# Cross-attention in layer 1 of a decoder: order of two score passes, and the places of the work around them

## The chip, the cores and the metric

The kernel is one program on one core of a Trainium2 chip. It is timed in microseconds (us) on the device, as the median of several executions; lower is better. A core has TensorE (matmuls, profile name PE, its weight loads PEld), VectorE (DVE), ScalarE (ACT), GpSimd (POOL) and SyncE (SP), each with a queue that it works through in order, and DMA engines that move data between the memories. Matmul results land in PSUM, which has banks of 512 float32 per partition; VectorE and ScalarE read them from there.

## The reference

The kernel computes a decoder of two layers on x of shape 4 x 512 x 512, each layer being self-attention, cross-attention and a feed-forward part with a layer norm after each. The change is in layer 1's cross-attention and in the preparation of the weights of the feed-forward part behind it. Cut to what is computed there:

```python
q = (x @ Wq).reshape(b, n, 32, 16)
k, v = jnp.split(ctx @ Wkv, 2, axis=-1)          # each reshaped to (b, ctx_n, 32, 16)
q = apply_axial_rope(q, pos_map)
k = apply_axial_rope(k, ctx_pos_map)
logits = jnp.einsum('bqhd,bkhd->bhqk', q, k) * scale
w = jax.nn.softmax(logits, axis=-1)
attn = jnp.einsum('bhqk,bkhd->bqhd', w, v)
x = layernorm(x + attn.reshape(b, n, 512) @ Wout + bout)

def quant_weight(w):                              # w_gate, w_up, w_down of the feed-forward part
    scale = jnp.mean(jnp.abs(w)) + EPS
    return jnp.clip(jnp.round(w / scale), -1.0, 1.0), scale
```

## The kernel before, in words

`l1_xattn` works on 4 batches (b) of 512 queries and 512 keys. The 32 heads of 16 channels are taken four at a time: a group `g` (32 in all) holds four heads, each in a strip of 32 partitions, of which 16 rows carry the head. Two groups make an `M` (16 in all, four to a batch), which share one projection of queries and keys. The scores are computed twice. `first_pass` (line 1178) makes scores with the queries along the partitions, and `row_maxes` (line 1182, VectorE) takes the negated maximum of each row. When the maxima of a group are there, `turn_maxes` transposes them (line 1187) and VectorE adds them to the queries as one more row (line 1188), so that `second_pass` (line 1194) makes scores with the keys along the partitions from which the maxima are already taken off. `exponentials` (line 1198, ScalarE) is then the plain exponential from PSUM to SBUF, and `values` (line 1205) multiplies it with the values and, by a column of ones, sums it.

The main loop in `run` has a step for each quarter (128 rows) of a group, 128 real steps in all, with a lead-in and an end. Each step has two halves. A half does the first pass for two of the four strips of the quarter five steps ahead, and the second pass for the other two strips of the present quarter. Each pass of a half takes one buffer of the pool `ps_b`, two banks wide; the pool has three buffers, handed out in turn, so a buffer is free for its third next user when VectorE's row maxes or ScalarE's exponential has read it. All other PSUM tiles of this stage come from the pool `ps_m`, two buffers of one bank, and one of them is held by the sum over four quarters that `values` builds up.

TensorE, VectorE and ScalarE keep the order in which the loop writes their instructions (`manual_schedule`); GpSimd and SyncE are put in order by the scheduler of the framework. The loop writes down, in each step, the two halves, and beside them what the dictionary `todo` holds for it. `plan(step, place, f, ...)` fills it: EARLY stands after the first half ahead of `values` of the step before, MIDDLE after those values, LATE after the second half. The entries that matter here:

- `project_queries`, `project_keys`: lines 1126 and 1140 on TensorE, copied out by ScalarE (1132, 1144), always LATE; `swap` and `rotate` then turn them by DMAs and GpSimd (1151 to 1161); `queries` (1166, ScalarE) and `keys` (1171, VectorE) mask them.
- `turn_residual`: transposes of the batch's x (1107), copied by ScalarE, and the bias added by GpSimd (1111).
- `prep_values`: the values' projection (line 160 is the helper `mm`), copied by ScalarE (1116).
- `gather` (ScalarE 1213 and 1214 for even groups, VectorE 1218 and 1219 for odd ones), `invert_sums` (transposes at 1225, reciprocals at 1229 on VectorE, a copy at 1231 on ScalarE) and `normalise` (transposes at 1238, product at 1243): the softmax's division.
- `out_projection`: one half of one tile of 128 rows in two parts of four matmul records each (1251), added to x by VectorE (1256), followed by the tile's statistics (219, 220); after a batch's last one GpSimd computes the inverse roots in a chain of small operations (227 to 234), and `normalise_tile` (239) uses them on VectorE.
- `quantized`: the three weights of the feed-forward part. In each of four chunks of 1 MB, loaded by SyncE (144), `add_up` sums the absolute values (1044); later `scale_of` adds the eight partial sums up on VectorE (1049) and over the partitions with a matmul (1051); then the chunks are loaded again and `round_off` scales half a chunk on VectorE (1062), clamps it on GpSimd (1063) and narrows it to bfloat16 on ScalarE (1064). Chunks take their buffers from the pool of ten weights, so a load waits until one is free.

Of the last real steps, those from 123 on have no first pass left. After the loop, the projections of batch 3 (entries of steps 130 to 137) and the feed-forward part follow.

Of the kernel before, what the change touches and what calls it, by code (L numbers as in the profile page):

```python
# [13 lines left out]
ALU = mybir.AluOpType  # L14
AX = mybir.AxisListType
# [71 lines left out]
def decoder_kernel(ctx: ExitStack, tc: tile.TileContext, a: dict, out: bass.AP):  # L87
# [21 lines left out]
    V, A, G, PE = nc.vector, nc.scalar, nc.gpsimd, nc.tensor  # L109
# [8 lines left out]
    def small(n, tag, bufs=2):  # L118
        return sp.tile([P, n], F32, tag=tag, name=tag, bufs=bufs)
# [15 lines left out]
    def psb():  # L135
        return pools["ps_b"].tile([P, 2, 512], F32, tag="b", name="ps_b")
# [33 lines left out]
    ones = cp.tile([P, P], F32, tag="ones", name="ones")  # L170
# [857 lines left out]
    def quantized(plan, name, n, sums_at, scale_at, rounds_at):  # L1028


        src = rows(a[name])
        per = 2048 // n
        got = {}

        def chunk(c):
            got["w"] = load(src[:, per * c:per * (c + 1), :], (per, n))

        def half(w, i):
            return w.rearrange("p k n -> p (k n)")[:, 1024 * i:1024 * i + 1024]

        def add_up(c, i):
            if c == 0 and i == 0:
                got["part"] = small(8, "part", 1)
            V.tensor_reduce(got["part"][:, 2 * c + i:2 * c + i + 1], half(got["w"], i), AX.X, ALU.add,
                            apply_absolute_value=True)

        def scale_of():
            row = small(1, "one", 8)
            V.tensor_reduce(row, got["part"], AX.X, ALU.add)
            ps = pst()  # L1050
            PE.matmul(ps[:, :1], lhsT=ones, rhs=row, start=True, stop=True)
            scale = cp.tile([P, 1], F32, tag=f"ws_{name}", name="ws")
            V.tensor_scalar(scale, ps[:, :1], 1.0 / (F * INNER), Q_EPS, ALU.mult, ALU.add)
            got["inv"] = cp.tile([P, 1], F32, tag=f"wi_{name}", name="wi")
            V.reciprocal(got["inv"], scale)
            wq = got["wq"] = [weight((2 * per, n), BF16) for _ in range(2)]
            quant[name] = chunks(wq[0]) + chunks(wq[1]), scale

        def round_off(c, i):
            w = half(got["w"], i)  # L1060
            dst = half(got["wq"][c // 2][:, per * (c % 2):per * (c % 2 + 1), :], i)
            V.tensor_scalar(w, w, got["inv"], ROUND, ALU.mult, ALU.add)
            G.tensor_scalar(w, w, ROUND + 1.0, ROUND - 1.0, ALU.min, ALU.max)
            A.activation(dst, w, AF.Copy, bias=-ROUND)

        for c in range(4):
            for at, f in ((sums_at, add_up), (rounds_at, round_off)):
                plan(at + 4 * c - 2 + (c == 0 and at == sums_at), LATE, chunk, c)
                for i in range(2):
                    plan(at + 4 * c + 2 * i, LATE, f, c, i)  # L1070
        plan(scale_at, EARLY, scale_of)


# [7 lines left out]
    def l1_xattn():  # L1081
# [92 lines left out]
        def first_pass(g, qi, half, s):  # L1174
            q, k = qk["q", g], qk["k", g]
            for j in range(2):
                i = 2 * half + j
                PE.matmul(s[:, j, :], lhsT=q[strip(i), tk(qi)], rhs=k[strip(i), :], start=True, stop=True)  # L1178

        def row_maxes(g, qi, half, s):  # L1180
            at = maxes[g % 2][:, qi, :].rearrange("p (i c) -> p i c", c=32)
            V.tensor_reduce(at[:, 2 * half:2 * half + 2, 16 * (1 - g % 2)], s, AX.X, ALU.max, negate=True)  # L1182
# [82 lines left out]
        def plan(step, place, f, *args):  # L1265
            todo.setdefault((step, place), []).append((f, args))
# [4 lines left out]
        for M in range(4 * B):  # L1271
            b, m, t0 = M // 4, M % 4, 8 * M
            if M:
                q, turn_q, turn_k = (-17, -13, -11) if M == 1 else (-21, -16, -13)
                for i in range(4):
                    plan(t0 + q + i, LATE, project_queries, M, i // 2, i % 2)
                plan(t0 + turn_q, EARLY, rotate, "q")
                for i in range(2):
                    plan(*(-5, EARLY) if M == 1 else (t0 - 17 + i, LATE), project_keys, M, i)
                plan(t0 + turn_k, EARLY, rotate, "k")  # L1280
            for par in range(2):
                plan(t0 - 10 + 2 * par if M else -9, EARLY, queries, M, par)
                plan(t0 - 7 + par if M else -9, EARLY, keys, M, par)
            for g in (2 * M, 2 * M + 1):
                plan(4 * g - 1, EARLY, turn_maxes, g)
                plan(4 * g + 4, MIDDLE, gather, g)
            if m == 0:
                if b:
                    plan(t0 - 23, EARLY, load_batch, b)
                    plan(t0 - 17, EARLY, angles)  # L1290
                    for k, x in enumerate(((-25, MIDDLE), (-23, EARLY), (-22, EARLY), (-21, MIDDLE))):
                        plan(t0 + x[0], x[1], turn_residual, b, k)
                for t, x in enumerate(((-3, MIDDLE), (-1, MIDDLE), (-1, MIDDLE), (1, EARLY))):
                    plan(t0 + x[0], x[1], prep_values, b, t)
            plan(t0 + 9 - (M == 4 * B - 1), LATE, invert_sums, M)
            plan(t0 + 10 - (M == 4 * B - 1), LATE, normalise, M)
            if m < 3:
                continue


            whole, pairs, norms = ((11, MIDDLE), (13, EARLY), (21, EARLY), (23, MIDDLE), (25, EARLY),
                                   (26, EARLY), (27, MIDDLE), (29, EARLY)), (), (33, 35, 37, 39)
            if b == B - 2:
                whole, pairs, norms = whole[:2], (19, 21, 23, 27, 29, 31), (34, 35, 36, 37)
            elif b == B - 1:
                whole, norms = [(10 + i, LATE) for i in range(8)], (18,) * 4
            for i, x in enumerate(whole):
                for part in range(2):
                    plan(t0 + x[0], x[1], out_projection, b, i // 2, i % 2, part)
            for i, x in enumerate(pairs, len(whole)):  # L1310
                for part in range(2):
                    plan(t0 + x + part, LATE, out_projection, b, i // 2, i % 2, part)
            for i in range(4):
                plan(t0 + norms[i], LATE, normalise_tile, b, i)
        for name, n, steps in (("L1_ffn_gateT", INNER, (2, 17, 19)), ("L1_ffn_upT", INNER, (35, 53, 54)),
# [22 lines left out]
        def run():  # L1338
            open_pools({"pp": (1, False), "ps_b": (3, True), "ps_m": (2, True)})
            st["wo"] = load(rows(a["L1_xattn_Wout"]), (4, F))  # L1340

            vv.extend(prob(f"vv{t}", [16, 48], 1) for t in range(4))
            for x in vv:
                G.memset(x[:, :, 16:32], 1.0)
            maxes.extend(prob(f"maxes{i}", [4, P], 1) for i in range(2))
            for x in maxes:
                G.memset(x, 0.0)

            N = 32 * B

            with tc.manual_schedule(engines={nc.tensor.engine, nc.vector.engine, nc.scalar.engine}):
                for step in range(min(x for x, _ in todo), max(x for x, _ in todo) + 1):
                    ahead, now, past = step + 5, step, step - 1
                    for half in range(2):
                        if 0 <= ahead < N:
                            s1 = psb()
                            first_pass(ahead // 4, ahead % 4, half, s1)
                        if 0 <= now < N:
                            s2 = psb()
                            second_pass(now // 4, now % 4, 1 - half, s2)  # L1360
                        if 0 <= ahead < N:
                            row_maxes(ahead // 4, ahead % 4, half, s1)
                        if 0 <= now < N:
                            exponentials(now // 4, now % 4, 1 - half, s2)
                        if half == 0:
                            for f, args in todo.get((step, EARLY), ()):
                                f(*args)
                            if 0 <= past < N:
                                values(past // 4, past % 4)
                            for f, args in todo.get((step, MIDDLE), ()):  # L1370
                                f(*args)
                    for f, args in todo.get((step, LATE), ()):
                        f(*args)
# [127 lines left out]
```

## Time and profile before

| what | value |
|---|---|
| median of 3 executions | 2916.74 us (2912.76 to 2916.99) |
| profiled execution, its own time | 2925.97 us |
| its span, first to last instruction | 2924.2 us |
| granted TensorE clock, mean | 0.983 |
| the stage of the edited loop | about 1970 to 2690 us of the span |
| busy in that stage (720 us) | TensorE 690.6, VectorE 458.5, ScalarE 366.2, GpSimd 198.5 |
| row maxes, line 1182 | 256 of 1.223 us |
| exponentials, line 1198 | 256 of 1.023 us |
| narrowing, line 1064 | 24 of 1.057 us |

A row of instructions names the line of the kernel, the engine, the operation, what it writes and reads with sizes, how often, the busy time in us and the mean in ns, and after a bar the idle time of the engine just before it with what ended that. A float32 matmul of the kernel appears as two records. A row of waits names who waited, for whom, and total us, times and longest. Records of TensorE that belong to different strips run at the same time and are counted once in busy time.

### The profile page before, as it was taken

The page shows a single profiled execution, that of the slowest core. Times are in us where ns is not written, and L with a number is a line of the kernel's source. Part 1 is how long each engine was busy: PE and PEld are TensorE (multiplying, and loading weights), DVE is VectorE, ACT ScalarE, POOL GpSimd, SP SyncE. Part 2 cuts the span into 40 slices and gives each one's busy share as a digit, 9 for nine tenths or more (in the row PEclk, how much of TensorE's full clock was granted, in tenths as well). Part 3 has the DMA queues.
Part 4 walks back from the last instruction along what each step waited for, and adds up shares of the span by engine and source line. Part 5 has one row for each costly group of instructions (what it writes and reads, how often), then busy time and mean ns, then how long its engine had stood idle before and what let it go on. Part 6 is the DMA issues. An engine that isn't in the chain of part 4 may idle for free. (4 is left out here: it accounts for less than half of the span.)

```text
span 2924.2 us, 30438 instructions
## 1 busy us (share of the span) xinstructions
PE 2763.2 (94%) x11434; PEld 1347.8 (46%) x11434; DVE 1757.1 (60%) x3551; ACT 1046.8 (36%) x1929; POOL 425.0 (15%) x436
## 2 busy tenths in 40 slices
PE   8999999998998889999999999999999999998987
PEld 3444444565665345555555555553334334334443
DVE  4565564553111476767667666756656666565998
ACT  2333342333221122232233223234555554554443
POOL 3000000042002100111101101123333232211000
PEclk9999999999999899999999999999999999999999
DMA  9700000004322120000000001111111020010000
GB/s 386 278 15 1 15 4 27 23 29 137 101 85 97 35 87 1 1 0 1 1 1 1 1 0 44 58 47 38 56 55 58 37 86 27 12 51 1 15 15 30
DMA packets 61128, 142.76 MB, mean 49 GB/s; under 512 B 6537, under 2 KB 26010, under 8 KB 54818
## 3 DMA queue, kind: packets, MB, share of 16 engines
q1 hardware_dynamic: 54818, 123.80, 11.8%
q0 software_dynamic: 6144, 16.79, 1.6%
q8 instruction: 99, 1.62, 0.2%
q14 instruction: 67, 0.55, 0.1%
HBM read 84.73 MB, written 47.45 MB: 45 GB/s over the span
## 5 line engine op out<-in xcount | busy, mean ns | idle before, releaser
L1182 DVE TENSOR_REDUCE maxes<-ps_b 128x2 f32<-128x1024 f32 x256 | 312.6, 1223 | 212.0 <-PE ps_b L1194 113.8
L160 PE MATMUL ps_m<-w,attnT 128*128 128x512 f32 (+1 forms) x992 | 391.8, 547 | 9.7 <-DVE x L313 9.7
L1198 ACT ACTIVATE PT<-ps_b 128x1024 f32<-128x1024 f32 x256 | 260.3, 1023 | 237.0 <-PE ps_b L1194 236.9
L1178 PE MATMUL ps_b<-k,q 32*128 32x512 f32 x1024 | 287.0, 642 | 6.8 <-ACT PT L1198 6.8
L1194 PE MATMUL ps_b<-q,k 32*128 32x512 f32 x1024 | 285.5, 642 | 1.4 <-DVE maxes L1182 1.4
L933 PE MATMUL ps_m<-xT,w 128*128 128x512 f32 x512 | 261.4, 594 | 0.0
L313 DVE TENSOR_TENSOR x<-x,ps_m 128x512 f32<-128x512 f32 x128 | 87.8, 687 | 284.5 <-PE ps_m L160 257.1
L160 PEld LDWEIGHTS ps_m<-w,attnT 128*128 128x128 f32 x736 | 141.2, 195 | 177.3 <-issue 162.8
L950 ACT ACTIVATE P<-ps_s,nmax 128x512 f32<-128x512 f32 (+3 forms) x256 | 135.4, 529 | 234.9 <-DVE nmax L948 233.8
L946 PE MATMUL ps_s<-k,q 128*128 128x512 f32 (+3 forms) x512 | 183.3, 441 | 19.1 <-POOL q L906 17.4
L906 POOL TENSOR_TENSOR q<-tmp 128x512 f32<-128x512 f32 x64 | 82.0, 1281 | 765.8 <-DVE tmp L905 731.2
L978 PE MATMUL ps_m<-PT,v 128*128 128x512 f32 (+3 forms) x512 | 162.8, 441 | 4.0 <-DVE PT L966 4.0
L370 ACT ACTIVATE P<-ps_s,nmax 128x512 f32<-128x512 f32 x128 | 88.5, 693 | 203.5 <-DVE nmax L368 203.5
L957 DVE TENSOR_SCALAR P<-P,sums 128x512 f32<-128x512 f32 (+3 forms) x256 | 152.0, 594 | 5.3
L1178 PEld LDWEIGHTS ps_b<-k,q 32*128 32x128 f32 x1024 | 76.5, 183 | 155.2 <-issue 141.1
L160 PE MATMUL ps_m<-w,xT 128*128 128x512 f32 (+1 forms) x384 | 143.8, 530 | 3.4 <-DVE v L338 3.4
L1205 PE MATMUL ps_m<-PT,vv 128*32 128x512 f32 x1024 | 137.5, 609 | 7.5 <-ACT PT L1198 7.5
L963 PEld LDWEIGHTS ps_t<-kc,P 128*128 128x128 f32 x640 | 84.0, 141 | 121.3 <-issue 82.0
L978 PEld LDWEIGHTS ps_m<-PT,v 128*128 128x128 f32 x512 | 89.0, 190 | 106.1 <-issue 48.8
L348 PE MATMUL ps_m<-xT,w 128*128 128x512 f32 x256 | 122.3, 605 | 10.4 <-DMA w<-in_L_attn_Wq 10.4
L948 DVE TENSOR_REDUCE nmax<-ps_s 128x1 f32<-128x512 f32 (+3 forms) x256 | 125.5, 490 | 5.6
L947 DVE TENSOR_TENSOR ps_s<-ps_s,mask 128x128 f32<-128x128 f32 x256 | 75.1, 294 | 81.1 <-PE ps_s L946 78.9
(281 smaller groups left out, 4403.7 us busy)
## 6 DMA issues: line engine op xcount, KB each, us to landing
hidden<-w SPq DMA_DIRECT2D x16, 1024.0 KB, 16.7
result<-w SPq DMA_DIRECT2D x16, 1024.0 KB, 16.3
w<-in_L_ffn_gateT SPq DMA_DIRECT2D x8, 1024.0 KB, 4.8
tmp<-tmp POOLq DMA_DIRECT2D x64, 128.0 KB
w<-in_L_ffn_upT SPq DMA_DIRECT2D x8, 1024.0 KB, 4.8
w<-in_L_ffn_downT SPq DMA_DIRECT2D x8, 1024.0 KB, 5.5
w<-in_L_attn_Wqkv SPq DMA_DIRECT2D x6, 1024.0 KB, 8.9
w<-in_L_attn_Wo SPq DMA_DIRECT2D x5, 1024.0 KB, 13.6
```

Source lines behind the costliest of these rows:

```text
L160: PE.matmul(ps, lhsT=x, rhs=y, start=(i == 0), stop=(i == n - 1))
L933: PE.matmul(ps_q[n], lhsT=wq[h // 4][:, i, tk(h % 4)], rhs=st["xt"][:, i, :], start=(i == 0), stop=(i == 3))
L946: PE.matmul(s[:, :w], lhsT=q[:, tk(qi)], rhs=k[:, :w], start=True, stop=True)
L948: V.tensor_reduce(nmax[:, qi:qi + 1], s[:, :w], AX.X, ALU.max, negate=True)
L950: A.activation(p[:, :w], s[:, :w], AF.Exp, bias=nmax[:, qi:qi + 1], accum_out=sums[:, qi:qi + 1])
L957: V.tensor_scalar(p[:, :w], p[:, :w], sums[:, qi:qi + 1], None, ALU.mult)
L978: PE.matmul(av[:, c * P:], lhsT=st["v"][:, c, tk(g)], rhs=pts[c][:, c * P:], start=(c == 0), stop=(c == 3))
L1178: PE.matmul(s[:, j, :], lhsT=q[strip(i), tk(qi)], rhs=k[strip(i), :], start=True, stop=True)
L1182: V.tensor_reduce(at[:, 2 * half:2 * half + 2, 16 * (1 - g % 2)], s, AX.X, ALU.max, negate=True)
L1194: PE.matmul(s[:, j, :], lhsT=k[strip(i), tk(c)], rhs=q[strip(i), :], start=True, stop=True)
L1198: A.activation(p, s, AF.Exp)
L1205: PE.matmul(avs[g][strip(i), :], lhsT=vv[c][:, 4 * m + i, 16 * par:16 * par + 32], rhs=pts[g, c, i // 2][:, i % 2, :], start=(c == 0), sto ...
```

## The change

Inside a half, the second pass now takes its buffer and is issued ahead of the first pass. From step 123 on, EARLY, `values` and MIDDLE stand behind the second half; before that they stay behind the first. The narrowing on ScalarE leaves `round_off` and becomes `narrow`, planned LATE one step later. The reduction of the eight partial sums leaves `scale_of` and becomes `row_sums`, LATE in the step before. The other plans are regrouped: the transposes of the residual and the half tiles of the output projection stand as pairs, EARLY and MIDDLE of the same step; three of the four value preparations of a batch move one to three steps later; for batch 2 the pieces spread over LATE places come first, and its last two half tiles move to steps 123 and 124 (from 99 and 101, which the first two had), with its four normalisations at steps 126 to 129 (from 122 to 125).

```diff
+        def row_sums():
+            got["row"] = small(1, "row", 1)
+            V.tensor_reduce(got["row"], got["part"], AX.X, ALU.add)
+
         def scale_of():
-            row = small(1, "one", 8)
-            V.tensor_reduce(row, got["part"], AX.X, ALU.add)
             ps = pst()
-            PE.matmul(ps[:, :1], lhsT=ones, rhs=row, start=True, stop=True)
+            PE.matmul(ps[:, :1], lhsT=ones, rhs=got["row"], start=True, stop=True)
...
             V.tensor_scalar(w, w, got["inv"], ROUND, ALU.mult, ALU.add)
             G.tensor_scalar(w, w, ROUND + 1.0, ROUND - 1.0, ALU.min, ALU.max)
+            got[c, i] = dst, w
+
+        def narrow(c, i):
+            dst, w = got.pop((c, i))
             A.activation(dst, w, AF.Copy, bias=-ROUND)
...
+        for c in range(4):
+            for i in range(2):
+                plan(rounds_at + 4 * c + 2 * i + 1, LATE, narrow, c, i)
+        plan(scale_at - 1, LATE, row_sums)
...
-                    for k, x in enumerate(((-25, MIDDLE), (-23, EARLY), (-22, EARLY), (-21, MIDDLE))):
+                    for k, x in enumerate(((-23, EARLY), (-23, MIDDLE), (-22, EARLY), (-22, MIDDLE))):
                         plan(t0 + x[0], x[1], turn_residual, b, k)
-                for t, x in enumerate(((-3, MIDDLE), (-1, MIDDLE), (-1, MIDDLE), (1, EARLY))):
+                for t, x in enumerate(((-3, MIDDLE), (1, EARLY), (1, MIDDLE), (2, EARLY))):
                     plan(t0 + x[0], x[1], prep_values, b, t)
...
-            whole, pairs, norms = ((11, MIDDLE), (13, EARLY), (21, EARLY), (23, MIDDLE), (25, EARLY),
-                                   (26, EARLY), (27, MIDDLE), (29, EARLY)), (), (33, 35, 37, 39)
+            whole, pairs, norms = [(x, y) for x in (13, 21, 25, 26) for y in (EARLY, MIDDLE)], (), (33, 35, 37, 39)
             if b == B - 2:
-                whole, pairs, norms = whole[:2], (19, 21, 23, 27, 29, 31), (34, 35, 36, 37)
+                whole, pairs, norms = ((35, EARLY), (36, EARLY)), (19, 21, 23, 27, 29, 31), (38, 39, 40, 41)
...
-                        if 0 <= ahead < N:
-                            s1 = psb()
-                            first_pass(ahead // 4, ahead % 4, half, s1)
                         if 0 <= now < N:
                             s2 = psb()
                             second_pass(now // 4, now % 4, 1 - half, s2)
                         if 0 <= ahead < N:
+                            s1 = psb()
+                            first_pass(ahead // 4, ahead % 4, half, s1)
                             row_maxes(ahead // 4, ahead % 4, half, s1)
                         if 0 <= now < N:
                             exponentials(now // 4, now % 4, 1 - half, s2)
-                        if half == 0:
+
+                        if half == (ahead >= N):
                             for f, args in todo.get((step, EARLY), ()):
```

## The prediction

> **What bounds the kernel now.** The page's engine table comes first: TensorE is busy 94% of the span.
>
> ```profile
> PE 2763.2 (94%) x11434; PEld 1347.8 (46%) x11434; DVE 1757.1 (60%) x3551; ACT 1046.8 (36%) x1929; POOL 425.0 (15%) x436
> ...
> L1182 DVE TENSOR_REDUCE maxes<-ps_b 128x2 f32<-128x1024 f32 x256 | 312.6, 1223 | 212.0 <-PE ps_b L1194 113.8
> ```
>
> The stage that is edited (1970 to 2690 us) has TensorE busy 690.6 of 720 us, which looks as if only 29 us could be won. The timeline says otherwise. A half step has a first pass (L1178, two strips) and a second pass (L1194, the other two strips), which run on TensorE side by side when both may start. Two half steps of TensorE (start, duration):
>
> ```profile
> 2209.60 0.70 PE L1178 MATMUL ps_b<-k,q 32*128 32x512 f32 x2
> 2209.62 0.70 PE L1194 MATMUL ps_b<-q,k 32*128 32x512 f32 x2
> ...
> 2210.68 0.70 PE L1140 MATMUL ps_m<-w 128*128 128x512 f32 x1
> ```
>
> ```profile
> 2201.27 0.70 PE L1178 MATMUL ps_b<-k,q 32*128 32x512 f32 x2
> 2201.59 0.70 PE L1194 MATMUL ps_b<-q,k 32*128 32x512 f32 x2
> ...
> 2202.65 0.64 PE L1205 MATMUL ps_m<-PT,vv 128*32 128x512 f32 x4
> ```
>
> In the first, both start together and the next work starts 1.07 us later. In the second, the second pass starts 0.32 late, and the next work 1.38 later. It is late because its bank (three buffers in turn) is that of the half before's first pass, and VectorE reads that one until 2200.31 + 1.23 = 2201.54:
>
> ```profile
> 2200.31 1.23 DVE L1182 TENSOR_REDUCE maxes<-ps_b 128x2 f32<-128x1024 f32 x1 [0.70 <-PE ps_b L1194]
> ```
>
> Over the 245 half steps where both passes run, I took from the records the start of the first L1194 less that of the first L1178: 63.5 us in all. In every one the end of the row maxes of the half before, plus 0.05, gives it within 0.1. TensorE shows as busy in that time. This is the wait that the change goes at; the answer for waits in this stage (total, times, longest) shows its visible part, and others:
>
> ```profile
> ACT w L1064 <- POOL w L1063: 54.9, 23, 5.4
> ...
> PEld ps_b L1194 <- DVE maxes L1182: 22.2, 47, 1.3
> ...
> PE ps_m L1205 <- ACT PT L1198: 7.5, 8, 2.0
> PE ps_b L1178 <- ACT PT L1198: 6.8, 5, 3.2
> ...
> PE ps_m L1051 <- DVE one L1049: 4.8, 3, 1.7
> ```
>
> In the last steps the chain of waits is a strict ring, 3.24 us a step (2672.20 to 2675.45, where the next exponential starts):
>
> ```profile
> 2672.20 1.03 ACT PT L1198
> ...
> 2673.28 1.06 PE ps_m L1205 x8
> 2674.34 1.08 PE ps_b L1194 x8
> ```
>
> **The swap.** With the second pass first, it takes the bank of the first pass two halves ago; its row maxes end at least 1.7 us before they are wanted in each of the 245 rows, so the VectorE wait is gone. In its place the first pass waits for the exponentials of the half before. Now: first pass start to row maxes' start 1.17 (2199.14, the record of the half before, to 2200.31), 1.23 of work, 0.05 to restart: 2.45. After: second pass start to exponentials' start 1.24 (2201.59 to 2202.83 in the same timeline), 1.02, 0.05: 2.31. The wait is what this exceeds the TensorE work between two half starts, 1.07 plus filler, and a wait in one half shortens the next one's. By the written plan each group of eight steps has six with a filler of 1.06 after the second half (distance 2.13) and two with the short transposes of 0.59 (distance 1.66). Now: 6 x 0.32 + 2 x 0.80 = 3.5 per eight steps; for 123 steps 54, and the measured 63.5 is 9 more because VectorE is late with other work. After: 6 x 0.18 + 2 x 0.65 = 2.38, for 123 steps 36.6. So -27 if ScalarE is never late.
>
> It will be late at times, and everything behind the first pass in TensorE's queue (values, fillers, next half) then waits: 16 copies of L1231, queued ahead of an exponential and held by VectorE's reciprocals, some 0.27 each (the exponential comes 0.77 late, against a half that starts 0.5 later than usual): 4.3; 32 gathering copies of 0.69 in 16 pairs, 0.15 a pair: 2.4; the 24 narrowed halves of 1.06 at 0.15: 3.6; copies of the residual's transposes, two to a step now, 3 x 0.45: 1.4. Sum 12, an estimate from those rows. Swap: -27 + 12 = **-15**. Bounds: -27 with none of it; with the exponentials' lateness left as it is, working down the table of halves gives 73.0 us of waits in place of 63.5, so +9.5.
>
> [...] Were it throughput, the order would buy nothing (0 in place of -15). But VectorE works 458.5 us of 720, 1.8 of each 2.66 us half: what binds is the round trip of one bank, and I go by the row. [...]
>
> **ScalarE's half of the rounding a step later.** No instruction is added; 24 activations (L1064) move. Now each is queued right after its clamp was asked for, so ScalarE stands 54.9 us for GpSimd with exponentials behind it. One step later ScalarE reaches each of them 2.9 us or more after its clamp's end in this trace (exponential's end of the next step less clamp's end, 24 rows), so the stand is gone. GpSimd's order changes a little: some of the later clamps stand behind two DMA issues of 0.57 each, and behind ScalarE's copy of the same step that these wait for, instead of before them; 2.9 - 1.15 is still cover; without it ScalarE waits the missing part. TensorE idles 7.5 + 6.8 = 14.3 on exponentials; 4.6 of it is in the ring at the end (1.23 + 3 x 1.11), 9.7 is this. I take **-8**, ends 0 and -9.7. The chunk's buffer comes free a step (5.3 us) later, and SP's loads queue for it. The tightest is the first down weight: issued 2354.89 after such an activation, first read by VectorE at 2375.35; 5.3 later and a landing of 4.8 to 5.5 leave some 10 us. Cost nothing.
>
> **Row sums a step earlier.** TensorE's scale matmul waited 4.8 us in three places for a reduction just queued. That small reduction (0.13) now runs a step before. **-4.6**, ends 0 and -4.8.
>
> **Last five steps.** Both halves come before values, so an exponential is hidden by the next 1.07 + 1.06 of TensorE work; ScalarE needs 2 x 1.02. The ring of 3.24 falls to about 2.14, four times: -4.4. Two quarter projections of batch 2 (2.0 us each) move here from steps 99 and 101: the same TensorE time, now in a place without idle, so nothing. Their statistics start the Newton chain on GpSimd at step 124 with the last clamp behind its first seven small operations (1.9 us) and 1.04 of its own; by my count it is ready when ScalarE comes, within 0.1, so up to 3 may be lost. **-3**, ends -4.6 and +1.5.
>
> **Regrouped fillers.** Projections, transposes and value preparations go as pairs around the values matmul. Instructions and time are equal. They cover fewer first-to-second-half waits, but in a run without cover those alternate 0.18 and 0, so the sum per step is the same. The second of a pair needs the bank that the first's copy leaves, about 2.1 us later; counted above for the transposes, else 0.
>
> **Sum.** -15 - 8 - 4.6 - 3 = -30.6. The profiled run took 2925.97 around a span of 2924.2; the median of three is 2916.74, 9 lower. The edits are in microseconds of a stage at granted clock 0.99, so I take them off the median: **2886**.
>
> **Rivals.** (1) *ScalarE takes over the bound*: the new waits swallow the swap's gain (swap 0, the end 0), the two others stay: -12.6, 2904. For: ScalarE is in order and has 0.45 us of other work per half; against: its row is shorter and the big block goes. (2) *Slower*: the moved activations still find the clamp unfinished, and now the first pass stands behind them. Going from no block to today's 55 us turns -27 into +9.5 at most; from -15 it is 0.45 us per us of block. With 24 blocks of 3.5 us (84): -15 + 38 - 4.6 - 3, about +15, 2932. It decides (+5.8) from 2.6 us per block, so a clamp 5.5 us later than now; against it is the 2.9 us cover. (3) *No change*: the second pass's wait is only handed over with the ends above cancelling, 2915; the 0.14 per step speaks against it. (4) *More*: ScalarE is never late and all idle goes: -46, 2871.
>
> **How the numbers follow.** A measurement of this kernel tells 0.2%, 5.8 us, from no change. Likeliest 0.65: 2886, its own range 2876 to 2897. (1) 0.20: 2904, from 2897 to 2911. (3) 0.05. (2) 0.07. (4) 0.03. Faster 0.88, same 0.05, slower 0.07. Range **2870 to 2907**: the end of case 4, and most of case 1.
>
> **What would show it.** Right: in full steps L1204 starts before L1188, the lag between them sums to 40 to 55 us, ends with an exponential and no longer with row maxes; no wait of the second pass for row maxes; the wait of the narrowing line for GpSimd near 0; no TensorE wait for the row sum; steps 124 to 127 near 2.2 us. Wrong: lags of over 0.5 us behind ScalarE in most steps, a wait of the narrowing line for its clamp of over 2 us, or VectorE late for the transposed maxes.

## The result and the profile after

The changed kernel takes 2866.76 us (median, 2864.58 to 2868.43) beside 2916.23 us for the kernel before (2912.76 to 2916.99): a ratio of 0.9832, 95% interval 0.9815 to 0.9849, or 49.5 us less. The forecast was 30.6 us less, and the time lies 3.2 us below the forecast range.

The page of the changed kernel, engine table and row maxes:

```profile
PE 2735.0 (95%) x11434; PEld 1333.5 (47%) x11434; DVE 1754.2 (61%) x3551; ACT 1047.2 (37%) x1929; POOL 422.4 (15%) x436
...
L1192 DVE TENSOR_REDUCE maxes<-ps_b 128x2 f32<-128x1024 f32 x256 | 312.5, 1223 | 179.1 <-PE ps_b L1188 178.5
```

The number of instructions on each engine is unchanged, and busy TensorE has shrunk by 28 us. That is no contradiction: where one pass waits while the other runs, TensorE counts as busy (in the stage 63.5 us before, 42.2 after), and at half clock it does too: from 2084.60 to 2088.00 of before it shows 3.40 us busy of 3.40 at a granted clock of 0.50. By the profile, VectorE now waits for the first pass (L1188) alone, no longer for the second as well.

The timeline of two half steps after the change (start, duration, instruction, and in brackets the wait before it):

```profile
2199.15 1.03 ACT L1208 ACTIVATE PT<-ps_b 128x1024 f32<-128x1024 f32 x1 [0.48 <-PE ps_b L1188]
...
2199.63 1.13 PE L1204 MATMUL ps_b<-q,k 32*128 32x512 f32 x4
2200.22 0.30 PEld L1188 LDWEIGHTS ps_b<-k,q 32*128 32x128 f32 x4 [0.30 <-ACT PT L1208]
2200.22 1.13 PE L1188 MATMUL ps_b<-k,q 32*128 32x512 f32 x4
...
2200.86 1.03 ACT L1208 ACTIVATE PT<-ps_b 128x1024 f32<-128x1024 f32 x1 [0.69 <-PE ps_b L1204]
```

The second pass (L1204) starts at once. The first pass starts 0.59 late, 0.04 after the exponential of the half before has ended (2199.15 + 1.03 = 2200.18). Over the 245 halves with both passes, this lag sums to 42.2 us (63.5 before). In all 245 the first pass starts right behind the second (in 72 of them) or, where the exponential of the half before ends later than that, 0.05 behind its end, within 0.1. The row maxes of two halves earlier, which hold the second pass's buffer, never delay it: the nearest end 0.37 before it starts.

The waits in the stage after (1963 to 2627 us; total, times, longest):

```profile
PEld ps_b L1188 <- ACT PT L1208: 14.5, 28, 1.5
...
ACT w L1070 <- POOL w L1065: 5.2, 4, 2.1
...
PE ps_b L1188 <- ACT PT L1208: 1.6, 5, 0.6
...
PE ps_m L1053 <- DVE row L1049: 0.8, 1, 0.8
...
PE ps_m L1215 <- ACT PT L1208: 0.6, 1, 0.6
```

ScalarE's stand for the clamp is down from 54.9 us to 5.2, TensorE's visible idle time on exponentials from 14.3 to 2.9, and the wait of the scale matmul from 4.8 to 0.8.

The last steps after the change, from the timeline:

```profile
2617.50 1.14 PE L1204 MATMUL ps_b<-q,k 32*128 32x512 f32 x8
...
2619.56 1.43 PE L1204 MATMUL ps_b<-q,k 32*128 32x512 f32 x8
...
2621.60 1.06 ACT L1070 ACTIVATE w<-w 128x1024 bf16<-128x1024 f32 x1 [0.88 <-POOL w L1065]
...
2623.62 1.13 PE L1204 MATMUL ps_b<-q,k 32*128 32x512 f32 x4 [0.57 <-ACT PT L1208]
...
2626.36 1.06 PE L1215 MATMUL ps_m<-PT,vv 128*32 128x512 f32 x8 [0.62 <-ACT PT L1208]
```

The ring of 3.24 us a step is now 2.06 (2617.50 to 2619.56), and 2.36 in the next step (to 2621.92). The last narrowing does come too early for its clamp, and costs 0.57 and 0.62 us behind it.

From both traces I made the same ledger. "Stage" runs from the first first-pass record to the end of the last second-pass record; "lags" is the sum of the starts of the later pass less those of the earlier; "idle" is TensorE's time without any record in the stage and in the wait of the last values just behind it (1.1 us before, 0.6 after); "half clock" is the time near the stage in which the granted clock was 0.5.

| us | before | after | difference |
|---|---|---|---|
| before the stage | 1974.8 | 1963.2 | -11.6 |
| stage | 707.1 | 661.6 | -45.5 |
| of it lags | 63.5 | 42.2 | -21.3 |
| idle | 26.5 | 6.8 | -19.7 |
| behind the stage | 242.3 | 240.3 | -2.0 |
| half clock | 13.6 | 0 | -13.6 |

The 11.6 us ahead of the stage arise where the two kernels have the same instructions; over the fourteen traces of this document that part lies anywhere between 1955 and 1978 us. The profiled execution of before was itself 9 us above its median, so the two spans are 59 us apart and the medians 49.5. What belongs to the change is the stage and a little behind it: 47.5 us. Two of the half-clock stretches, 3.4 us each, lay inside the stage; work in them took nearly twice as long (the values at 2084.88 us 1.93 in place of 1.06), so about 3.4 us was lost there, by estimate. With lags and idle time that makes 44.4, of which 0.5 lies just behind the stage, beside its 45.5.

### The profile page after: what moved, and what is told of

Same layout as the page of the kernel before. It is cut to its first block, busy times and chain, and to the rows that moved or that the text cites. A ratio compares the mean times of both kernels' runs of the same rounds, so it can differ in the third digit from the quotient of the medians.

```text
span 2865.0 us, 30441 instructions
## 1 busy us (share of the span) xinstructions
PE 2735.0 (95%) x11434; PEld 1333.5 (47%) x11434; DVE 1754.2 (61%) x3551; ACT 1047.2 (37%) x1929; POOL 422.4 (15%) x436
## 4 chain that ended last, share of the span: by engine, by line
PE 53%; DVE 10%; POOL 2%; issue 1%; ACT 1%; DMA 0%; POOLq 0%; DVEq 0%; ACTq 0%
PE ps_m L160 16%; PE ps_b L1204 7%; PE ps_m L933 6%; PE ps_s L946 5%; PE ps_m L1215 4%; PE ps_t L963 2%; PE ps_m L978 2%; PE ps_m L1136 2%; PE ps_b L1188 2%; PE ps_m L1261 2%; POOL q L906 1%; DVE P L1430 1%; PE ps_m L1150 1%; PE ps_s L160 1%; DVE tmp L905 1%
## 5 line engine op out<-in xcount | busy, mean ns | idle before, releaser
L160 PE MATMUL ps_m<-w,attnT 128*128 128x512 f32 (+1 forms) x992 | 384.3, 539 | 0.0
L1188 PE MATMUL ps_b<-k,q 32*128 32x512 f32 x1024 | 286.3, 640 | 1.7 <-ACT PT L1208 1.6
L1204 PE MATMUL ps_b<-q,k 32*128 32x512 f32 x1024 | 283.6, 639 | 0.6 <-ACT PT L1208 0.6
L946 PE MATMUL ps_s<-k,q 128*128 128x512 f32 (+3 forms) x512 | 183.3, 441 | 18.5 <-POOL q L906 16.8
L1204 PEld LDWEIGHTS ps_b<-q,k 32*128 32x128 f32 x1024 | 75.9, 183 | 147.4 <-issue 119.1
## 6 DMA issues: line engine op xcount, KB each, us to landing
hidden<-w SPq DMA_DIRECT2D x16, 1024.0 KB, 16.9
```

Source lines behind the costliest of these rows:

```text
L160: PE.matmul(ps, lhsT=x, rhs=y, start=(i == 0), stop=(i == n - 1))
L946: PE.matmul(s[:, :w], lhsT=q[:, tk(qi)], rhs=k[:, :w], start=True, stop=True)
L1204: PE.matmul(s[:, j, :], lhsT=k[strip(i), tk(c)], rhs=q[strip(i), :], start=True, stop=True)
```

## The experiments

The kernels of one group below ran on one chip together with the kernel before, whose median was 2929.06 in the first group, 2928.89 in the second, 2911.47 in the third and 2910.95 in the fourth. So times are compared by ratio, and the stages by the ledger.

| run | ratio, 95% interval | stage | lags | idle | half clock |
|---|---|---|---|---|---|
| before (the trace above) | 1 | 707.1 | 63.5 | 26.5 | 13.6 |
| after (the trace above) | 0.9832 (0.9815 to 0.9849) | 661.6 | 42.2 | 6.8 | 0 |
| swap alone | 1.0018 (1.0000 to 1.0036) | 716.7 | 61.2 | 36.5 | 37.4 |
| narrowing alone | 0.9962 (0.9945 to 0.9978) | 699.0 | 65.6 | 18.5 | 10.2 |
| all but the swap | 0.9909 (0.9888 to 0.9930) | 686.7 | 68.4 | 4.6 | 6.8 |
| narrowing put back | 0.9957 (0.9945 to 0.9970) | 699.0 | 65.6 | 22.1 | 23.8 |
| last steps put back | 0.9846 (0.9827 to 0.9864) | 664.9 | 42.2 | 9.9 | 0 |
| fillers put back | 0.9863 (0.9847 to 0.9880) | 671.7 | 42.0 | 16.8 | 0 |
| short holes | 0.9896 (0.9877 to 0.9916) | 681.5 | 42.1 | 16.4 | 3.4 |
| long holes | 1.0083 (1.0055 to 1.0112) | 736.2 | 41.3 | 50.9 | 61.2 |
| half tiles late | 0.9840 (0.9822 to 0.9858) | 663.4 | 35.0 | 13.9 | 0 |
| and values late | 0.9860 (0.9843 to 0.9877) | 667.7 | 33.2 | 18.1 | 6.8 |
| some half tiles late | 0.9808 (0.9791 to 0.9825) | 654.8 | 35.5 | 6.0 | 0 |
| after, again | 0.9823 (0.9804 to 0.9843) | 661.1 | 42.2 | 6.3 | 0 |

### The swap alone (kernel before, with this edit)

```diff
-                        if 0 <= ahead < N:
-                            s1 = psb()
-                            first_pass(ahead // 4, ahead % 4, half, s1)
                         if 0 <= now < N:
                             s2 = psb()
                             second_pass(now // 4, now % 4, 1 - half, s2)
                         if 0 <= ahead < N:
+                            s1 = psb()
+                            first_pass(ahead // 4, ahead % 4, half, s1)
```

> The kernel before with the two score passes exchanged and nothing else; the narrowing stays right behind its clamp. Theory (the parts need each other): the first pass now stands behind ScalarE's blocks of some 2.3 us, so the lags between the passes sum to about 73 us in place of 63.5, and the time is 5 to 12 us above the kernel before, 2921 to 2928 us. Rival (the exchange carries the gain by itself): lags near 42 us as in the changed kernel, some 21 us faster, about 2895 us.

Measured: 1.0018, about 5 us slower, with an interval that begins at 1. From the waits of its stage:

```profile
ACT w L1064 <- POOL w L1063: 59.0, 23, 5.5
...
PEld ps_b L1178 <- ACT PT L1198: 28.9, 38, 2.7
```

The second pass's wait for row maxes is gone (the nearest end 0.63 us before it starts), the first pass's wait for exponentials has taken its place, and ScalarE still stands 59 us for the clamp. The lags are 61.2, less than expected, but TensorE's visible idle time has grown by 10.0. So the swap by itself buys nothing: it moves the dependence onto the engine that is blocked.

### The narrowing alone, and the narrowing put back

The first is the kernel before with `narrow` split from `round_off` and planned a step later; the second is the changed kernel with that undone:

```diff
-            got[c, i] = dst, w
-
-        def narrow(c, i):
-            dst, w = got.pop((c, i))
             A.activation(dst, w, AF.Copy, bias=-ROUND)
...
-        for c in range(4):
-            for i in range(2):
-                plan(rounds_at + 4 * c + 2 * i + 1, LATE, narrow, c, i)
```

> The kernel before with the narrowing a step later and nothing else. Theory: the lags stay at 63.5 us, since they hang on VectorE; TensorE's idle time behind exponentials of 9.7 us goes, and with it the two stretches at half clock at 2085 and 2136 us (3.4 us each, worth 3.4 us together), if these follow from TensorE's idle time: 10 to 13 us faster, about 2904 us. Rival (ScalarE's blocks are hidden and the half clock has another cause): under 4 us faster, and the half clock stays.

> The changed kernel with the narrowing again right behind its clamp, in the same step. Theory: 24 blocks of about 2.3 us stand ahead of exponentials on which the first pass now waits: lags 42 to about 75 us, some idle time and half clock back, 30 to 40 us slower than the changed kernel, 2897 to 2907 us. Rival (the two parts are independent): slower by what the narrowing alone is worth, 10 to 13 us, about 2879 us.

Alone it gives 0.9962, 11 us; the stage is 8.1 us shorter, its idle time 8.0 lower, its lags 2.1 higher. The two half-clock stretches at 2085 and 2136 us are gone, as expected, but one of 3.4 us stands in the last steps, where the kernel before has none. Taken out of the changed kernel it costs far more: 0.9957 in place of 0.9832, 36 us, with 37.4 us in the stage. From the waits with it put back:

```profile
ACT w L1066 <- POOL w L1065: 62.1, 24, 4.4
...
PEld ps_b L1181 <- ACT PT L1201: 32.5, 42, 4.1
```

The same stand of ScalarE now lands on the first pass: lags 65.6 in place of 42.2, idle 22.1 in place of 6.8, of which 11.7 is the first pass waiting for an exponential, and 23.8 us at half clock.

### All but the swap (the changed kernel, with the first pass in front again)

```diff
+                        if 0 <= ahead < N:
+                            s1 = psb()
+                            first_pass(ahead // 4, ahead % 4, half, s1)
                         if 0 <= now < N:
                             s2 = psb()
                             second_pass(now // 4, now % 4, 1 - half, s2)
                         if 0 <= ahead < N:
-                            s1 = psb()
-                            first_pass(ahead // 4, ahead % 4, half, s1)
```

> The changed kernel with the first pass again in front of the second. Theory (sum of separate waits): lags back to about 60 us, all else as in the changed kernel: 18 to 22 us slower than it, about 2887 us. Rival (the regrouped plan only works with the exchange): 30 us slower or more, 2897 us or above.

Measured: 0.9909, about 22 us slower than the changed kernel. From its waits:

```profile
PEld ps_b L1204 <- DVE maxes L1192: 26.3, 52, 1.7
```

With everything else done, idle time is down to 4.6, but the second pass is late behind row maxes again, 68.4 us in all. Adding the swap takes 25.1 us off the stage. In stage time against the kernel before: the swap alone +9.6, all else alone -20.4, both together -45.5, so 34.7 us belong to neither part by itself.

### The last steps put back (changed kernel)

```diff
-                        if half == (ahead >= N):
+                        if half == 0:
```

> The changed kernel with the early places and the values again behind the first half in the last five steps too. Theory: a ring of exponential, values and scores of about 3.2 us a step is back in steps 124 to 127, 3 to 5 us of idle time, and with it perhaps a half-clock stretch worth 2 to 3 us more: 3 to 8 us slower than the changed kernel. Rival (the two projections moved there fill the ring): under 2 us.

Measured: the stage is 3.3 us longer, nearly all of it idle time (9.9 against 6.8), in which the values wait for exponentials four times, 4.6 us in all, as in the kernel before. The ratio, 0.9846, cannot tell this from nothing; the trace does.

### The fillers put back (changed kernel)

```diff
-                    for k, x in enumerate(((-23, EARLY), (-23, MIDDLE), (-22, EARLY), (-22, MIDDLE))):
+                    for k, x in enumerate(((-25, MIDDLE), (-23, EARLY), (-22, EARLY), (-21, MIDDLE))):
...
-                for t, x in enumerate(((-3, MIDDLE), (1, EARLY), (1, MIDDLE), (2, EARLY))):
+                for t, x in enumerate(((-3, MIDDLE), (-1, MIDDLE), (-1, MIDDLE), (1, EARLY))):
...
-            whole, pairs, norms = [(x, y) for x in (13, 21, 25, 26) for y in (EARLY, MIDDLE)], (), (33, 35, 37, 39)
+            whole, pairs, norms = ((11, MIDDLE), (13, EARLY), (21, EARLY), (23, MIDDLE), (25, EARLY),
+                                   (26, EARLY), (27, MIDDLE), (29, EARLY)), (), (33, 35, 37, 39)
```

> The changed kernel with the residual's transposes, the value preparations and the output projections of batches 0, 1 and 3 at their old places; batch 2's projections stay at the new ones. Theory (equal work, lags alternate between 0.18 and 0 whether covered or not): within 3 us of the changed kernel, the lead-in longer by 3.4 us and the main part shorter by as much. Rival (the regrouping carries part of the gain that the forecast missed): 6 us slower or more.

Measured: 0.9863, about 9 us slower than the changed kernel, the stage 10.1 longer and its idle time 10.0 higher, at the same lags. My theory was wrong here and the rival right. TensorE's own waits in this run:

```profile
PE ps_m L1117 <- DVE q L1198: 3.6, 6, 1.0
PE ps_m L1261 <- DVE q L1198: 3.4, 7, 1.0
PE ps_m L160 <- ACT vv L1126: 2.0, 3, 0.7
...
PE ps_m L160 <- DVE q L1198: 1.2, 3, 0.4
```

and one of them in its timeline:

```profile
2052.99 0.66 PE L1197 MATMUL ps_m<-kc,maxes 128*128 128x128 f32 x4
...
2053.57 1.07 PE L1215 MATMUL ps_m<-PT,vv 128*32 128x512 f32 x8
2053.77 1.22 DVE L1192 TENSOR_REDUCE maxes<-ps_b 128x2 f32<-128x1024 f32 x1
2054.91 0.68 DVE L1198 TENSOR_TENSOR q<-q,ps_m 128x512 f32<-128x512 f32 x1
...
2055.64 0.66 PE L1117 MATMUL ps_m<-kc,x 128*128 128x128 f32 x4 [1.00 <-DVE q L1198]
```

`turn_maxes` stands EARLY and its transposes (L1197) fill the one free bank of `ps_m`; the other is held by the sum of `values`. VectorE empties the bank only behind a row maxes, at 2054.91 + 0.68 = 2055.59. The filler in MIDDLE of the same step needs that bank and stands 1.00 us. `turn_maxes(g)` is at step 4g - 1, and the old plan puts seven pieces into MIDDLE of exactly such steps: offsets -25, -21, 11, 23 and 27 leave 3 when divided by 4, and so does -1, which carried two value preparations one behind the other (they move by two steps, the fourth by one). The new offsets (13, 21, 25, 26, -23, -22, 1, 2) avoid all of these steps. In the kernel before the same two waits came to 3.7 and 2.0 us; with the swap alone they were 8.0 and 2.1. So the swap lets more of them show, and the regrouping removes most of them (0.2 and 0.7 are left). Why they show more behind the swap I have not traced further.

### Holes in TensorE's work (changed kernel)

Both kernels add, at eight steps, a matmul that fills a bank of `ps_m`, a number of passes of VectorE over it (1 or 7), and a matmul that waits for them, with nothing of the reference's computation changed. They ask whether idle time costs more than itself.

```diff
+        def hole(n):
+            ps, t = psm(), small(1, "hole", 2)
+            PE.matmul(ps, lhsT=ones, rhs=st["wo"][:, 0, :], start=True, stop=True)
+            for _ in range(n):
+                V.tensor_scalar(ps, ps, 0.5, None, ALU.mult)
+            V.tensor_copy(t, ps[:, :1])
+            PE.matmul(ps[:, :1], lhsT=ones, rhs=t, start=True, stop=True)
+
+        for s in (44, 52, 60, 68, 76, 84, 92, 100):
+            plan(s, LATE, hole, 1)          # 7 in the second kernel
```

> The changed kernel with an added hole for TensorE at eight steps of the stage (44 to 100, every eighth): a matmul into PSUM, one VectorE pass of 512 columns over it, a copy, a small matmul that waits for it. Results that the kernel hands out are unchanged. Expected 8 x about 1 us of idle TensorE and 8 x about 1 us of added matmuls, 12 to 20 us slower than the changed kernel, and no half-clock stretch by either theory.

> The same eight holes with seven VectorE passes each, so that TensorE idles about 5 us in each. Theory (TensorE's own idle time brings the half clock): a stretch of 3.4 us or more at half clock follows in most holes, at 1.7 us of lost time for each 3.4, so the kernel is 8 x 4 us longer than with short holes and 8 to 14 us beyond that. Rival (the half-clock stretches fall by chance): none or one in the stage, and only the idle time is added.

The short holes idle TensorE 1.16 us each, the long ones 5.56. From short to long the stage grows by 54.7 us and TensorE's idle time by only 34.5. Three stretches around the first long hole (length, busy us and instructions of each engine, then the granted clock, DMA share and GB/s):

```profile
2216.70:2223.50 6.80, 1.42 (x6) 0.54 (x4) 5.81 (x9) 0.92 (x2) 0.00 (x0) 1.00 0.00 0
2223.50:2230.30 6.80, 6.80 (x22) 3.73 (x26) 1.65 (x2) 1.02 (x1) 0.00 (x0) 0.50 0.00 0
2230.30:2237.10 6.80, 6.80 (x44) 3.00 (x36) 4.00 (x6) 1.83 (x2) 0.00 (x0) 1.00 0.01 2
```

and inside the second, the half tile (1.99 us at full clock) and the values (1.07):

```profile
2226.02 3.78 PE L1261 MATMUL ps_m<-w,attnT 128*128 128x256 f32 x8
2229.73 1.34 PE L1215 MATMUL ps_m<-PT,vv 128*32 128x512 f32 x8
```

Behind each of the eight long holes the clock was 0.5 for 6.8 to 10.2 us, 61.2 in all; behind none of the short ones. (Their kernel's one stretch of 3.4 us begins at 2481.6, 29 us after the last hole before it; ahead of it a first pass started 1.9 us late, held by an exponential.) The lags are no longer (41.3). The 20.2 us that idle time does not explain, more than the 8 to 14 expected, are 2.5 for each hole, or 0.35 us for each added us at half clock (57.8). The kernel before had 13.6 us at half clock and the changed one none; at that rate it is 4.8 us.

### Fillers moved between the halves (changed kernel, three attempts)

What is left in the stage is mostly the lag of 42.2. A filler that stands LATE, between the two halves, covers a lag of the first pass. Of the lags after the change, nine are over 0.8 (11.4 us together), nineteen between 0.45 and 0.8 (11.3), and the other 217 sum to 19.6. The first attempt moves the half tiles of batches 0 and 1 there, the second two value preparations of each batch as well:

```diff
-            whole, pairs, norms = [(x, y) for x in (13, 21, 25, 26) for y in (EARLY, MIDDLE)], (), (33, 35, 37, 39)
+            whole, pairs, norms = [(x, LATE) for x in (17, 18, 25, 26, 33, 34, 41, 42)], (), (43, 44, 45, 46)
```

> The changed kernel with the half tiles of the output projection of batches 0 and 1 (2.0 us each, sixteen of them) moved from their pairs around the values to the late place of the steps whose only late filler is a short transpose of 0.59 us; their layer-norm steps move some steps later. Theory (a lag is the round trip of 2.31 us less the distance between two half starts, so it goes where the filler is longest missing): the lag of about 0.65 us at sixteen places goes, lags 42 to 32 us, 5 to 9 us faster than the changed kernel, about 2860 us on its chip. Rival (the lag is set by ScalarE's other work, whatever the distance): lags within 3 us of 42 and no gain.

> As the one before, and two of the four value preparations of each batch (2.0 us each) also in the late place of the two such steps at the start of the batch, ahead of the transposes. Theory: three or four batches x two places x about 0.5 us more off the lags, 2 to 4 us faster than the one before, unless the transposes then wait for the bank that ScalarE empties. Rival: the bank of the preparation is emptied late, TensorE idles there, and it is level or slower.

The lags fell as expected, to 35.0 and 33.2, and the time did not: 0.9840 and 0.9860. The first attempt's TensorE waits show the price:

```profile
PE ps_m L1248 <- DVE x L1266: 4.1, 8, 0.5
PE ps_m L1235 <- DVE x L1266: 4.1, 8, 0.5
```

The transposes of `invert_sums` and `normalise`, LATE in the same steps, now follow a half tile directly and stand 0.51 us each, sixteen times, until VectorE has added that tile to x and freed its bank. That is 8.2 us of new idle time for 7.2 of lag. In the second attempt half tiles and transposes also wait 4.1 us for ScalarE's copies of the value projections, as its rival had it.

The third attempt moves four half tiles of each of the two batches only, and takes the transposes that they met out of the way, with the changed kernel run again beside it:

```diff
-            plan(t0 + 9 - (M == 4 * B - 1), LATE, invert_sums, M)
-            plan(t0 + 10 - (M == 4 * B - 1), LATE, normalise, M)
+            where = MIDDLE if M in (5, 6, 9, 10) else LATE
+            plan(t0 + 9 - (M == 4 * B - 1), where, invert_sums, M)
+            plan(t0 + 10 - (M == 4 * B - 1), where, normalise, M)
...
-            whole, pairs, norms = [(x, y) for x in (13, 21, 25, 26) for y in (EARLY, MIDDLE)], (), (33, 35, 37, 39)
+            whole, pairs, norms = [(x, y) for x in (13, 21) for y in (EARLY, MIDDLE)], (), (36, 37, 38, 39)
+            whole += [(x, LATE) for x in (25, 26, 33, 34)]
```

> The changed kernel, with the half tiles that stood as pairs EARLY and MIDDLE of the 25th and 26th step moved one by one to LATE of steps 25, 26, 33 and 34 in batches 0 and 1 (so that they stand between second half and first half, where a wait of the first pass for the exponentials would show), and with invert_sums and normalise of the same batches' Ms that met them there put in MIDDLE. Theory (the rest of the stage's loss is the lag of the first pass, 42 us, and work between the halves covers it): lags about 38 in place of 42, and no new wait for the bank of ps_m, so 2 to 5 us faster than the changed kernel, ratio about 0.982. Rival: the transposes in MIDDLE now wait for the bank there (0.5 us each as in the first try, where it was the x add that held it), TensorE idle in the stage 10 or more in place of 6.8, and the time level with the changed kernel or above it.

> The changed kernel itself, on the same chip as the run beside it, so that the two can be compared without the step between chips: ratio 0.983 by its first measurement; its lags and idle time as in its own trace, 42 and 7 us.

Measured: 2855.25 us (2851.60 to 2858.36) beside 2861.74 (2854.08 to 2863.34) for the changed kernel; ratios to the kernel before 0.9808 and 0.9823, whose intervals overlap. The ledger is clearer: the stage is 6.3 us shorter (654.8 against 661.1), the lags 6.7 lower, idle time 6.0 against 6.3. TensorE's waits have no row for the x add at these transposes any more; the only wait on it left is one of 0.5 us at L1197, which the changed kernel has too.

So in this pair a shorter lag does become stage time, us for us, once no bank is paid for it. The table says the same of the other runs: in its six runs without half clock, what is left of the stage after lags and idle time is 612.6 to 614.5 us. This is the best version here, 6.5 us below the changed kernel by the medians.

## Why the prediction fell short

The direction and the mechanism of the swap were right. Three terms were not: one was too small, and two were put at nothing. The stage and what lies behind it gave 47.5 us against the 30.6 forecast; of the 16.9 missing, the swap makes 6.3, the fillers 3.1 net, and the half clock up to 5.4. About 2 stay unassigned.

| step of the prediction | forecast | measured |
|---|---|---|
| the swap | -15 (lags 63.5 to 48.6) | lags -21.3 (to 42.2) |
| narrowing a step later | -8 | -8.0 (idle on exponentials outside the last steps, 9.7 to 1.7) |
| row sums a step earlier | -4.6 | -4.1 (4.8 to 0.8) |
| last five steps | -3 | -3.4 (4.6 to 1.2); put back, +3.3 |
| regrouped fillers | 0 | about -4.7 against before (5.7 to 1.0); put back, +10.1 |
| half clock | not considered | about -3.4 in the stage, up to -2.0 behind it |

*The swap.* The term that was mis-sized is "ScalarE late", 12 us, put on top of the clean 36.6. The lags came to 42.2, so ScalarE's lateness cost 5.6. It is concentrated: the nine lags over 0.8 exceed the clean 0.65 by 5.5 together, three of them in the first four steps and five where a narrowed half stands ahead of the exponential or of the one before. The many small copies that I charged with 0.15 to 0.45 each show no such sum: the other 236 lags are near the clean pattern. The row arithmetic behind the clean part (2.31 us against a distance of 1.66 or 2.13) held. Had VectorE's throughput been the bound, the order would have been worth nothing; in the kernel with everything else done the swap takes 25.1 us off the stage. The two round trips read from the rows, 2.45 us before and 2.31 after, differ by 0.14 us a step, the figure that case (3) leans on, or 17 us over 123 steps; the lags fell by 21.3.

*Swap and narrowing together.* The bound that I kept, +9.5 for the swap while ScalarE stays blocked, was measured as +9.6 in the stage. The agreement is partly luck: I expected 73 us of lags, and it was 61.2 of lags, 10.0 more idle time, and more half clock. What counts for the forecast is that the two edits must be costed in order: first the block, then the swap.

*Regrouped fillers.* This is the step that failed outright: "The second of a pair needs the bank that the first's copy leaves ...; counted above for the transposes, else 0". I looked at what the new pairs might wait for and not at what the old places were waiting for already. The trace of before had it. Among its waits the weight loads (PEld) of these fillers stand: half tiles 9.8 us and transposes 7.5 for VectorE's add to q, value projections 4.5 for ScalarE's copy. TensorE's own rows are these:

```profile
PE ps_m L160 <- ACT vv L1116: 2.0, 3, 0.7
PE ps_m L1107 <- DVE q L1188: 2.0, 4, 0.7
...
PE ps_m L1251 <- DVE q L1188: 1.2, 3, 0.7
```

With waits too short for a row they are 5.7 us of the 26.5 idle. New waits on the x add and on the products of `normalise`, together 1.6 more than before, take part of it back.

*Half clock.* I wrote that the edits are in microseconds "at granted clock 0.99" and left it there. The missing 0.01 was 13.6 us in three stretches, each behind idle time that the change removes or shortens. The last of them, behind the stage, is in part chance: "and values late" has the changed kernel's last steps and yet 3.4 us at half clock there, with 241.3 us behind its stage, where "half tiles late" has none and 239.8.

*Row sums.* No run puts them back alone; their 4.1 us are read from the two traces.

*The rivals.* ScalarE as the bound (2904) is out: the swap's gain was not swallowed but larger. The slower case needed a block of 2.6 us at each narrowing; the block left is 5.2 us in four places, longest 2.1. The case "more" (2871) comes nearest in size, but not by its way, since ScalarE is late still and 6.8 us of idle time remain. The range left out a gain from the fillers because I had put no bound on that step at all, only a zero.

*The signs.* Second pass first, lags within 40 to 55 and ended by exponentials, no wait for row maxes, last steps near 2.2 us: all seen. The wait of the scale matmul is 0.8, not none.

## What to carry to other kernels

An engine's busy share can hide the very wait that bounds a stage (TensorE showed 690.6 us busy of 720 here, 63.5 of it lags): where two parts run side by side, compare their starts and see which reader's end gives them. When a change hands a dependence from one engine to another, cost it after removing that engine's blocks, since the swap and all the rest were worth +9.6 and -20.4 us apart and -45.5 together. And when fillers are moved, read what they wait for in their old places as carefully as what they may meet in the new ones: with the two banks of `ps_m`, a filler directly behind another's result paid for the emptying, 0.5 to 1.0 us each time here.

## What the runs showed of the hardware

TensorE's clock fell to half behind short idle times. The kernel before, around its first scale matmul (the same columns as above):

```profile
2081.20:2084.60 3.40, 1.75 (x9) 0.60 (x10) 3.19 (x5) 1.61 (x2) 1.11 (x2) 1.00 0.35 75
2084.60:2088.00 3.40, 3.40 (x18) 0.98 (x18) 0.32 (x2) 0.00 (x0) 0.00 (x0) 0.50 0.77 311
```

An idle time of 1.65 us, with TensorE busy for 1.75 of 3.4 us, was followed by 3.4 us at half clock. All stretches at half clock near the stage last 3.4, 6.8 or 10.2 us in these traces, and 3.4 us of which TensorE was busy for half were enough ahead of this one. None of the eight short holes, 1.16 us on average, had such an effect, and all eight of 5.56 us did. So a wait of TensorE cost more than its own length here: 2.5 us more behind each of the long holes.

What decided in these traces, by the estimate that follows, was less the length of an idle time than how much of one stretch it takes. In each of the fourteen traces all half-clock stretches begin whole multiples of 3.41 us apart. I cut the stage and the 12 us behind it by that grid, and counted TensorE's work in each piece so that a pass that only waits behind the other does not count (each record of a strip at 0.134 us, an eighth of the 1.07 of a half without lag). Of the 34 pieces at full clock with less than 1.67 us of work, 30 were followed by half clock; of the 2759 with more, none. By this estimate about half a piece without work was enough, and a lag counted as idle time: the piece above has 1.15 us of work, not 1.75, and the piece ahead of the stretch in the kernel with the short holes has 1.55, with no hole in it. The long holes, 5.4 us and more, take at least 2.7 us out of one piece wherever they fall. The changed kernel escapes narrowly, since its poorest piece in the stage has 1.71 us of work.
